# Attention scores of two heads' groups in one pair of PSUM banks: clips, exponentials and additions of 896 elements instead of 448

## The chip, the core and the metric

The kernel runs on one core of one Trainium2 chip. The metric is device time in microseconds (us), the median of several runs. Five engines work side by side, each through its own queue in order: TensorE (PE in the profile, with its weight loads as PEld), VectorE (DVE), ScalarE (ACT), GpSimd (POOL) and SyncE (SP), which here only starts transfers. Matmul results land in PSUM, in eight banks of 512 fp32 elements per partition; DVE and ACT read them from there.

## The reference

Two transformer layers over 8 sequences of 112 tokens, 512 wide, with a context of 375 positions for each sequence:

```python
x = x + _L0_xattn_ref(_layernorm(x), ctx_2048, ctx_2048, mask_bool)
x = x + _L0_ffn_ref(_layernorm(x), w1, w2, w3)
x = x + _L1_xattn_ref(_layernorm(x), ctx_2048, mask_int, Wq, bq, Wk, ...)
x = x + _L1_ffn_ref(_layernorm(x), wq_gate, s_gate, wq_up, s_up, ...)
```

The change is in the third line, the second layer's attention with 16 heads of 32:

```python
q, k, v = proj(hs, Wq, bq), proj(at, Wk, bk), proj(at, Wv, bv)
scores = jnp.clip(jnp.einsum('bhsd,bhtd->bhst', q, k) / sqrt(32), -50, 50)
scores = jnp.clip(jnp.where(attend, scores, -10000.0), -50, 50)
probs = softmax(scores)
delta = rs * (einsum('bhst,bhtd->bhsd', probs, v) @ Wo.T + bo)
```

followed by a layer norm of delta with gamma and beta. The mask is applied by the upper bound of the clip: 50 where a position counts, -50 where it doesn't.

## The kernel before

The kernel goes through four parts: the first attention and first feed-forward (up to about 212 us of the profiled span), the queries of the second attention (to 236), the second attention (236 to 396), and the second feed-forward (to the end). TensorE and SP run in the order in which the program is written throughout; in the attention stage all five engines do.

**Keys and values** of a sequence come in seven steps, each one fill of a bank by TensorE (L194 for keys, L203 for values) and a copy out of it (L197, L205 on ACT in this stage). The generator `key_value_steps` hands them out one at a time, and `fill` puts one behind each step of the attention as other work for TensorE. They use `ps_mm`, a pool of two banks, which the projection (L800) and the turning of its result (L841) use too.

**One step of the attention** is a batch `b` (8 of them) and a third `c` of the 375 positions, 125 each. `scores` takes four banks, one for each of four 32-row groups of the array, `r`; each holds four heads' groups (`dc`) of 112 columns, 448 elements. The matmuls (L902) go `dc` outside, `r` inside. For each bank, DVE clips it into a tile in SBUF (L907) and ACT takes the exponential in place (L908). The four banks are the whole of the pool `ps_s`, so the next step's matmuls need the banks that this step's clips free.

**Sums.** One step later `sums` multiplies the exponentials with the values (L928, into the one bank `num`). The softmax's denominators need the exponentials summed over all 375 positions: POOL adds the second third's to the first's in place (L894, in `add`; on DVE for the last batch), at the start of step `c == 2`, and matmuls with ones take the sum of that and of the last third (L923, into `den`). Then ACT copies both out (L934, L935), and in the next batch's step `c == 1` `divide` takes the reciprocal (L939) and multiplies (L941) on DVE, behind that step's clips.

**Projection and normalisation** of token block `b - 2` follow at `c == 2`: L800 on TensorE, then on DVE and POOL a chain (L806, L143 and on, `rsqrt_pool` at L102 to L109, L812, L813, L819, L821 to L824) whose last part runs before the clips of the next batch's steps. L834 and L841 turn the normalised block for the second feed-forward. Beside this, integer weights arrive by DMA in pieces of 640 columns in two buffers (`load_integers`) and are converted by ACT (L877) and POOL (L879) in `convert_integers`, at set steps, ahead of the exponentials in ACT's queue; a buffer is free for the next DMA when POOL is done.

**Other users of `ps_s`.** In the queries, `less` (L741, read by DVE at L745) and the turning of normalised blocks (L227, `transpose2`); in the second feed-forward, `gate` and `up` (L1031), a bank each for 128 of 1408 hidden rows: ACT reads `gate` (L1036), DVE multiplies with `up` (L1037), and TensorE is two such blocks of rows ahead at most, since there are four banks. In that part the order on DVE, ACT and POOL is the scheduler's.

Of the kernel before, what the change touches and what calls it, by code (L numbers as in the profile page):

```python
# [23 lines left out]
F32 = mybir.dt.float32  # L24
# [6 lines left out]
ALU = mybir.AluOpType  # L31
AX = mybir.AxisListType
PSUM = bass.MemoryType.PSUM
ENGINES = mybir.EngineType

P = 128
B, T, D = 8, 112, 512
KC = D // P
S2, CK = 375, 125
NCK = S2 // CK  # L40
# [3 lines left out]
GROUPS = [(0, 4), (4, 7)]  # L44
HD = 32
NR = P // HD
# [10 lines left out]
CLIP = 50.0 / SC1  # L57
# [7 lines left out]

SPLIT = 2.0 ** -12
LESS = 1.0 - 2.0 ** -13


@with_exitstack  # L70
def two_layers(ctx: ExitStack, tc: tile.TileContext, x, ctxT, ctxN, mask0, mask1, w1, w2, w3,
               wq, wk, wv, wo, bq, bk, bv, bo, gamma, beta, rscale,
               wg, sg, wu, su, wd, sd, out):
    nc = tc.nc
# [72 lines left out]
    def normaliser(srcs, name):  # L147

        mv = moments(srcs, name)
        r = srcs[0].shape[0]  # L150
        ve = small[-1].tile([P, len(srcs)], F32, name=f"{name}_ve", bufs=1)[:r]
        nc.vector.tensor_scalar_add(ve, mv[:, :, 1], LN_EPS)
        rstd = rsqrt(ve, name)

        def write(h, j):
            nc.vector.tensor_scalar(h, srcs[j], mv[:, j, 0:1], rstd[:, j:j + 1],
                                    ALU.subtract, ALU.mult)
        return write
# [59 lines left out]
    def write2(i, write, j, pool):  # L218
        h2[i] = pool.tile([P, D], F32, name="d", bufs=2)
        write(h2[i], j)  # L220

    def transpose2(i, psum):

        g = 0 if i < GROUPS[0][1] else 1
        pt = psum.tile([P, KC, P], F32, name="s")
        for kc in range(KC):
            nc.tensor.transpose(pt[:, kc, :], h2[i][:, kc * P:(kc + 1) * P], ident)  # L227
        j = i - GROUPS[g][0]
        high, low, diff = (t[:, :, j * P:(j + 1) * P] for t in h2T[g])
        nc.scalar.activation(high, pt, AF.Identity, scale=LESS)  # L230

        def end():
            nc.vector.tensor_sub(low, pt, high.bitcast(F32))
            nc.vector.scalar_tensor_tensor(diff, high.bitcast(F32), SPLIT, low.bitcast(F32),
                                           ALU.mult, ALU.subtract)
        return end


    with tc.tile_pool(name="w0", bufs=1, side="right") as w0p, \
# [290 lines left out]
        with tc.tile_pool(name="work1", bufs=2, side="right") as work1:  # L530
# [90 lines left out]
            for i in range(2, NT):  # L621
# [51 lines left out]
                elif i == 4:  # L673
# [3 lines left out]
                                                 for name in ("wq_high", "wq_low", "h2T_high"))  # L677
                    nc.scalar.activation(wq_high, wq_s, AF.Identity, scale=LESS)
                    nc.gpsimd.tensor_sub(wq_low, wq_s, wq_high.bitcast(F32))
# [22 lines left out]

    tailp = ctx.enter_context(tc.tile_pool(name="tailp", bufs=1, side="right"))

    ps_s = ctx.enter_context(tc.tile_pool(name="ps_s1", bufs=4, space=PSUM))
    ps_mm = ctx.enter_context(tc.tile_pool(name="ps_mm1", bufs=2, space=PSUM))
    kv_psum[0] = ps_mm

# [11 lines left out]
    upper = tailp.tile([CK, NCK, B], F32, name="upper")  # L720
# [44 lines left out]
    with tc.tile_pool(name="g1p", bufs=1, side="right") as g1p:  # L765
        h2T[1] = [g1p.tile([P, KC, 384], F32R, name=f"h2T1_{k}") for k in range(3)]
        write = normaliser(xs[4:6], "ln2b")
        for i in range(4, 6):
            write2(i, write, i - 4, tailp)
            transpose2(i, ps_s)()  # L770
        next(asking)
        write2(6, normaliser(xs[6:], "ln2c"), 0, tailp)
        transpose2(6, ps_s)()
        for g in range(2):
            for _ in asking:
                pass
            asking = queries(1)
# [59 lines left out]
    def transpose4(i, pool, name):  # L837

        pt = pool.tile([P, KC, P], F32, name=name)
        for kc in range(KC):  # L840
            nc.tensor.transpose(pt[:, kc, :], h4[i][:, kc * P:(kc + 1) * P], ident)  # L841
        j = i - GROUPS[0 if i < GROUPS[0][1] else 1][0]
        hi, lo = (h4T[k][:, :, j * P:(j + 1) * P] for k in range(2))
        nc.scalar.copy(hi, pt)
        return lambda: nc.vector.tensor_sub(lo, pt, hi.bitcast(F32))


    with tc.tile_pool(name="work2", bufs=1, side="right") as work2, \
# [21 lines left out]
        def convert_integers():  # L870
            for raw, which, half, c, n in loaded:
# [12 lines left out]

        sets = [[work2.tile([P, KC, T], F32, name=f"e{i}{r}") for r in range(NR)]
                for i in range(NCK)]

        def add(b):  # L890
            add = (nc.gpsimd if b in ADD_POOL else nc.vector).tensor_add
            for r in range(NR):
                e, e1 = (sets[(b + c) % NCK][r][:CK] for c in range(2))
                add(e, e, e1)  # L894

        def scores(b, c):
            kT = kvs_of[b][0]
            ss = [ps_s.tile([CK, KC, T], F32, name="s") for r in range(NR)]
            for dc in range(KC):
                for r in range(NR):  # L900
                    rows = slice(r * HD, (r + 1) * HD)
                    nc.tensor.matmul(ss[r][:, dc, :], lhsT=kT[rows, dc, c * CK:(c + 1) * CK],  # L902
                                     rhs=qT[rows, dc, b * T:(b + 1) * T], start=True, stop=True)
            es = sets[(b + c) % NCK]
            for r in range(NR):
                e = es[r][:CK]
                nc.vector.tensor_scalar(e, ss[r], upper[:, c, b:b + 1], -CLIP, ALU.min, ALU.max)  # L907
                nc.scalar.activation(e, e, AF.Exp, scale=SC1)  # L908
            return es

# [37 lines left out]
        for b in range(B):  # L950
            for c in range(NCK):
                if c == 2 and b in ADD_POOL:
                    add(b)
                if (b, c) in due:
                    convert_integers()
                    if counts:
                        load_integers(counts.pop(0))
                es = scores(b, c)
                if c == 2 and b not in ADD_POOL:
                    add(b)  # L960
                if c < STEPS[b]:
                    fill(1)
                if c == NCK - 1:
                    sums(*last)
                if (b, c) == (B - 1, NCK - 1):
                    over = tailp.tile([P, 29], F32, name="over")
                    nc.gpsimd.tensor_scalar(over, squares, WIDE, 1.0, ALU.is_gt, ALU.mult)
                if b == 0 and c > 0:
                    next(folding)
                if c == 0:  # L970
                    while later:
                        later.pop()()
                    if b >= 3:
                        project_end(b - 3)
                elif c == 1 and b >= 1:
                    divide(b - 1)
                elif c == 2:
                    turned = 3 <= b < 3 + GROUPS[0][1]
                    if turned:
                        write4(b - 3)  # L980
                    if b >= 2:
                        project_product(b - 2)
                    if b == B - 1:

                        hits = ps_s.tile([1, 29], F32, name="s")
                        nc.tensor.matmul(hits, lhsT=ones[:, :1], rhs=over, start=True, stop=True)
                        wide = tailp.tile([1, 1], I32, name="wide")
                        nc.vector.tensor_reduce(wide, hits, AX.X, ALU.max)
                    if b >= 2:
                        project_begin(b - 2)  # L990
                    if turned:
                        later.append(transpose4(b - 3, ps_mm, "mm"))
                if last and c < NCK - 1:
                    sums(*last)
                last = b, c, es
# [8 lines left out]
    with tc.tile_pool(name="work3", bufs=2, side="right") as work3, \  # L1004
# [49 lines left out]
        def feed_forward1():  # L1054
            gus = [work3.tile([P, HC, 512], F32R, name=f"gu_{k}", bufs=1) for k in range(2)]
            gate_up1(0, 0, 2, gus)
            project(NT - 1)
            gate_up1(0, 2, HC, gus)
            for i in range(*GROUPS[0]):
                if GROUPS[1][0] + i < NT:  # L1060
                    write4(GROUPS[1][0] + i)
                down1(0, i, gus)
                if GROUPS[1][0] + i < NT:
                    transpose4(GROUPS[1][0] + i, ps_s, "s")()
            gus = [work3.tile([P, HC, 512], F32R, name=f"gu_{k}", bufs=1) for k in range(2)]
            gate_up1(1, 0, HC, gus)
            for i in range(*GROUPS[1]):
                down1(1, i, gus)

        def feed_forward1_wide(g):  # L1070
# [27 lines left out]
            for i in range(i0, i1):  # L1098
# [5 lines left out]
                                     start=(hc == 0), stop=(hc == HC - 1))  # L1104
                finish(i, ps)

        is_wide = nc.values_load(wide[0:1, 0:1], min_val=0, max_val=P)
        with tc.If(is_wide == 0) as fits:
            feed_forward1()
        with fits.Else():  # L1110
            project(NT - 1)
            feed_forward1_wide(0)
            for i in range(*GROUPS[1]):
                write4(i)
                transpose4(i, ps_s, "s")()
            feed_forward1_wide(1)


def _laid_out(inputs):
# [63 lines left out]
```

## Time and profile before

| what | us |
|---|---|
| median of 3 runs (517.44 to 518.0) | 517.8 |
| the profiled execution, its own time | 517.36 |
| its span in the profile | 515.6 |

Busy time of the engines by stretch, from the windows of the trace (us):

| stretch | length | PE | DVE | ACT | POOL |
|---|---|---|---|---|---|
| 200 to 236, queries | 36 | 35.18 | 25.53 | 14.11 | 6.06 |
| 236 to 260 | 24 | 23.69 | 13.65 | 17.17 | 8.06 |
| 260 to 280 | 20 | 19.87 | 13.88 | 14.13 | 8.04 |
| 280 to 300 | 20 | 20.00 | 13.04 | 8.82 | 8.82 |
| 320 to 340 | 20 | 19.02 | 17.80 | 11.80 | 11.69 |
| 340 to 360 | 20 | 20.00 | 16.15 | 11.74 | 12.89 |
| 360 to 380 | 20 | 19.46 | 17.40 | 12.74 | 14.08 |
| 380 to 400 | 20 | 19.78 | 16.43 | 10.62 | 8.17 |

A busy TensorE in such a row is not TensorE at its peak: a matmul's record lasts until its modelled end, so a wait in the middle of a group shows as a group that lasts longer than its like, not as idle time. A line of the profile names the line of the program, the engine, the operation, the tiles written and read with their shapes, and the number of instructions; what follows depends on the view and is said there. The granted TensorE clock is 1.00 in all of these stretches.

### The profile page before, as it was taken

Reading aid. Unit: us, or ns where it says so; the run is one execution under the profiler, and the core shown is the slowest. Engines: PE = TensorE matmul, PEld = TensorE weight load, DVE = VectorE, ACT = ScalarE, POOL = GpSimd, SP = SyncE. Lnnn points to the kernel's source line nnn. Section 1 sums busy time; section 2 is a strip of 40 time slices with the busy share of each in tenths; the row PEclk is TensorE's granted clock in tenths of the full one; section 3 lists DMA queues with packets and bytes.
Section 4 is the critical chain, followed back from the end, with each engine's and each line's share of the span. In section 5 each row is a group of like instructions: output and inputs, shape, how many; then the busy total and the mean of one; then the engine's idle time right before and its main releaser. Section 6 shows DMA issues by size and latency. Waiting matters only on the chain.

```text
span 515.6 us, 8804 instructions
## 1 busy us (share of the span) xinstructions
PE 502.3 (97%) x3380; PEld 315.0 (61%) x3380; DVE 334.3 (65%) x801; ACT 252.4 (49%) x438; POOL 133.9 (26%) x221
## 2 busy tenths in 40 slices
PE   9999999999999999999999999999999999999995
PEld 6445554455545455686565465555555788889983
DVE  3642548767798986964676588997897753334432
ACT  0326656857565665336675375465665233103310
POOL 0000121110011164211551475574753430000000
PEclk9999999999999999999999999999999999999998
DMA  8997795200120100122421112012320000010001
GB/s 242 363 407 298 274 326 201 79 18 0 61 82 1 60 2 0 37 109 58 162 70 53 61 52 62 3 53 62 98 76 5 21 1 1 20 42 20 1 20 46
DMA packets 13343, 45.75 MB, mean 89 GB/s; under 512 B 2081, under 2 KB 3120, under 8 KB 12144
## 3 DMA queue, kind: packets, MB, share of 16 engines
q1 hardware_dynamic: 11744, 41.43, 23.4%
q0 software_dynamic: 1248, 3.70, 2.2%
q8 instruction: 28, 0.46, 0.4%
q14 instruction: 19, 0.16, 0.1%
q10 hardware_dynamic: 304, 0.01, 0.0%
HBM read 41.46 MB, written 1.84 MB: 84 GB/s over the span
## 4 chain that ended last, share of the span: by engine, by line
PE 47%; DVE 6%; POOL 2%; DMA 1%; ACT 1%; issue 1%; DVEq 0%; POOLq 0%
PE s L1031 14%; PE mm L203 8%; PE down L1049 7%; PE mm L800 4%; PE s L902 3%; PE num L928 2%; PE mm L194 2%; DVE e L907 2%; PE den L923 2%; DMA raw<-in_wd_dram 1%; PE mm L737 1%; PE mm L735 1%; PE s L741 1%; DVE e L939 1%; POOL ln_t L108 1%
## 5 line engine op out<-in xcount | busy, mean ns | idle before, releaser
L194 PE MATMUL mm<-cT,wk 128*128 128x375 f32 x256 | 87.6, 487 | 0.0
L203 PE MATMUL mm<-wv,cT 128*125 128x512 f32 x192 | 87.6, 599 | 0.0
L1031 PE MATMUL s<-h4T,w 128*128 128x512 f32 (+1 forms) x352 | 72.6, 367 | 0.2 <-PE num L928 0.2
L1031 PEld LDWEIGHTS s<-h4T,w 128*128 128x128 f32 x352 | 63.5, 188 | 8.8 <-PE num L928 0.5
L907 DVE TENSOR_SCALAR e<-s,upper 125x448 f32<-125x448 f32 x96 | 59.0, 676 | 14.7 <-PE s L902 13.9
L908 ACT ACTIVATE e<-e 125x448 f32<-125x448 f32 x96 | 51.7, 570 | 27.6 <-DVE e L907 27.0
L194 PEld LDWEIGHTS mm<-cT,wk 128*128 128x128 f32 x256 | 47.0, 191 | 27.6 <-issue 0.8
L203 PEld LDWEIGHTS mm<-wv,cT 128*125 128x125 f32 x192 | 34.5, 187 | 38.0 <-issue 36.4
L894 POOL TENSOR_TENSOR e<-e,e 125x448 f32<-125x448 f32 x28 | 33.7, 1233 | 14.9 <-PE num L928 14.9
L1049 PE MATMUL down<-w,gu 128*128 128x512 f32 x154 | 37.0, 396 | 0.0
L541 PE MATMUL mm<-w_q,q_qT 128*128 128x512 fp8e4 (+1 forms) x168 | 34.6, 361 | 1.5 <-ACT q_qT L352 1.1
L439 POOL DMA_DIRECT2D tokens<-x x14 | 10.7, 768 | 90.6 <-DVE x L433 64.0
L1049 PEld LDWEIGHTS down<-w,gu 128*128 128x128 f32 x154 | 28.6, 188 | 6.7
L1039 ACT CAST gu<-gu 128x512 fp32r<-128x512 f32 (+1 forms) x22 | 12.5, 567 | 39.6 <-DVE gu L1037 39.6
L877 ACT ACTIVATE w<-raw,zero_point 128x640 fp32r<-128x640 int32 (+2 forms) x29 | 22.6, 781 | 18.9 <-DMA raw<-in_wd_dram 7.6
L570 POOL TENSOR_SCALAR q<-gu 128x704 bf16<-128x704 f32 x14 | 10.8, 787 | 80.0 <-ACT gu L567 80.0
L902 PE MATMUL s<-qT,kv 32*125 32x112 f32 x768 | 29.3, 280 | 0.6 <-DVE qT L745 0.3
L1037 DVE SCALAR_TENSOR_TENSOR gu<-s,su,gu 128x512 f32<-128x512 f32 (+1 forms) x22 | 15.0, 684 | 21.9 <-PE s L1031 20.6
L902 PEld LDWEIGHTS s<-qT,kv 32*125 32x125 f32 x768 | 24.5, 183 | 7.1 <-issue 5.6
L541 PEld LDWEIGHTS <-q_qT 128*128 128x128 bf16 x168 | 16.4, 98 | 20.3 <-issue 1.8
L879 POOL TENSOR_SCALAR w<-raw 128x640 fp32r<-128x640 int32 (+2 forms) x29 | 19.8, 693 | 34.2 <-ACT w L877 33.9
L800 PE MATMUL mm<-wo,qT 128*128 128x512 f32 x56 | 25.8, 603 | 1.0 <-DVE qT L941 1.0
(236 smaller groups left out, 787.5 us busy)
## 6 DMA issues: line engine op xcount, KB each, us to landing
cT<-in_ctxT_dram SPq DMA_DIRECT2D x13, 750.0 KB, 6.1
raw<-in_w_dram SPq DMA_DIRECT2D x6, 1408.0 KB, 19.2
cN<-in_ctxN_dram SPq DMA_DIRECT2D x8, 768.0 KB, 4.4
raw<-in_wg_dram SPq DMA_DIRECT2D x8, 320.0 KB, 3.1
raw<-in_wu_dram SPq DMA_DIRECT2D x8, 320.0 KB, 3.0
raw<-in_wd_dram SPq DMA_DIRECT2D x8, 320.0 KB, 3.1
out_dram<-d SPq DMA_DIRECT2D x7, 256.0 KB, 2.0
wk<-in_wk_dram SPq DMA_DIRECT2D x4, 256.0 KB, 4.8
```

What stands on the lines that cost most here:

```text
L194: nc.tensor.matmul(ps[dc], lhsT=wk_s[:, kc, dc * P:(dc + 1) * P], rhs=cT[:, kc, :], start=(kc == 0), stop=(kc == KC - 1))
L203: nc.tensor.matmul(ps, lhsT=cT[:, kc, c * CK:(c + 1) * CK], rhs=wv_s[:, kc, :], start=(kc == 0), stop=(kc == KC - 1))
L541: nc.tensor.matmul(ps[:, :n], lhsT=qT[:, kc, :], rhs=w[:, kc * H + n0:kc * H + n0 + n], start=(kc == 0), stop=(kc == KC - 1))
L800: nc.tensor.matmul(ps, lhsT=qT[:, kc, i * P:(i + 1) * P], rhs=wo_s[:, kc, :], start=(kc == 0), stop=(kc == KC - 1))
L877: nc.scalar.activation(t, raw, AF.Square, bias=zero_point, accum_out=squares[:, k:k + 1])
L879: nc.gpsimd.tensor_scalar(t, raw, -128.0, 1.0, ALU.add, ALU.mult)
L894: add(e, e, e1)
L902: nc.tensor.matmul(ss[r][:, dc, :], lhsT=kT[rows, dc, c * CK:(c + 1) * CK], rhs=qT[rows, dc, b * T:(b + 1) * T], start=True, stop=True)
L907: nc.vector.tensor_scalar(e, ss[r], upper[:, c, b:b + 1], -CLIP, ALU.min, ALU.max)
L908: nc.scalar.activation(e, e, AF.Exp, scale=SC1)
L1031: nc.tensor.matmul(ps[:, :n], lhsT=w[:, c:c + P], rhs=h4T[k][:, kc, :n], start=(kc == 0 and k == 0), stop=(kc == KC - 1 and k == 1))
L1049: nc.tensor.matmul(ps, lhsT=gus[k][:, hc, j * P:(j + 1) * P], rhs=w[:, c:c + D], start=(hc == 0 and k == 0), stop=(hc == HC - 1 and k == 1))
```

## The change

Two PSUM banks become one tile, a pair, and `ps_s` becomes a pool of two pairs in place of four banks. In `scores`, rows groups 0 and 1 go into one pair, 2 and 3 into the other; the matmuls and their order stay. One clip, one exponential and one addition take a pair, 896 elements. The exponentials' tiles are laid out in twos to match, and single heads' parts of them are views. Counts fall from 96 to 48 clips and exponentials, from 28 to 14 additions on POOL and from 4 to 2 on DVE.

Everything else that used `ps_s` asks a small class `Halves`, which takes a pair from the pool and hands out its two banks one after the other. There are two of them, one for `less`, `gate` and `up`, one for turned blocks; a half that is left over is dropped at the border of a stage. A pair is free for its next user when all that read either half are done.

```diff
+class Halves:
+    def __init__(self, pool):
+        self.pool, self.left = pool, []
+
+    def tile(self, shape, dtype, name):
+        if not self.left:
+            pair = self.pool.tile([P, 2, 512], F32, name="s")
+            self.left = [pair[:, 0, :], pair[:, 1, :]]
+        n = 1
+        for d in shape[1:]:
+            n *= d
+        t = self.left.pop(0)[:shape[0], :n]
+        return t if len(shape) == 2 else t.rearrange("p (a b) -> p a b", a=shape[1])
...
-    ps_s = ctx.enter_context(tc.tile_pool(name="ps_s1", bufs=4, space=PSUM))
+    ps_pair = ctx.enter_context(tc.tile_pool(name="ps_s1", bufs=2, space=PSUM))
+    ps_s, ps_turned = Halves(ps_pair), Halves(ps_pair)
...
-            transpose2(i, ps_s)()
+            transpose2(i, ps_turned)()
...
-        sets = [[work2.tile([P, KC, T], F32, name=f"e{i}{r}") for r in range(NR)]
+        twos = [[work2.tile([P, 2, KC, T], F32, name=f"e{i}{h}") for h in range(NR // 2)]
                 for i in range(NCK)]
+        sets = [[two[r // 2][:, r % 2] for r in range(NR)] for two in twos]
+        ps_turned.left.clear()
 
         def add(b):
             add = (nc.gpsimd if b in ADD_POOL else nc.vector).tensor_add
-            for r in range(NR):
-                e, e1 = (sets[(b + c) % NCK][r][:CK] for c in range(2))
+            for h in range(NR // 2):
+                e, e1 = (twos[(b + c) % NCK][h][:CK] for c in range(2))
                 add(e, e, e1)
 
         def scores(b, c):
             kT = kvs_of[b][0]
-            ss = [ps_s.tile([CK, KC, T], F32, name="s") for r in range(NR)]
+            ss = [ps_pair.tile([P, 2, 512], F32, name="s") for h in range(NR // 2)]
             for dc in range(KC):
                 for r in range(NR):
                     rows = slice(r * HD, (r + 1) * HD)
-                    nc.tensor.matmul(ss[r][:, dc, :], lhsT=kT[rows, dc, c * CK:(c + 1) * CK],
+                    nc.tensor.matmul(ss[r // 2][:CK, r % 2, dc * T:(dc + 1) * T], lhsT=kT[rows, dc, c * CK:(c + 1) * CK],
                                      rhs=qT[rows, dc, b * T:(b + 1) * T], start=True, stop=True)
-            es = sets[(b + c) % NCK]
-            for r in range(NR):
-                e = es[r][:CK]
-                nc.vector.tensor_scalar(e, ss[r], upper[:, c, b:b + 1], -CLIP, ALU.min, ALU.max)
+            for h in range(NR // 2):
+                e = twos[(b + c) % NCK][h][:CK].rearrange("p a k t -> p a (k t)")
+                nc.vector.tensor_scalar(e, ss[h][:CK, :, :KC * T], upper[:, c, b:b + 1], -CLIP,
+                                        ALU.min, ALU.max)
                 nc.scalar.activation(e, e, AF.Exp, scale=SC1)
-            return es
+            return sets[(b + c) % NCK]
...
-                        hits = ps_s.tile([1, 29], F32, name="s")
+                        hits = Halves(ps_pair).tile([1, 29], F32, name="s")
...
-                    transpose4(GROUPS[1][0] + i, ps_s, "s")()
+                    transpose4(GROUPS[1][0] + i, ps_turned, "s")()
...
+        for halved in ps_s, ps_turned:
+            halved.left.clear()
```

More of the change, by code (lines that the diff above doesn't have):

```diff
@@ L769, in two_layers @@
             write2(i, write, i - 4, tailp)
-            transpose2(i, ps_s)()
+            transpose2(i, ps_turned)()
         next(asking)
         write2(6, normaliser(xs[6:], "ln2c"), 0, tailp)
-        transpose2(6, ps_s)()
+        transpose2(6, ps_turned)()
         for g in range(2):
@@ L1109, in two_layers @@
             feed_forward1()
+            for halved in ps_s, ps_turned:
+                halved.left.clear()
         with fits.Else():
@@ L1114, in two_layers @@
                 write4(i)
-                transpose4(i, ps_s, "s")()
+                transpose4(i, ps_turned, "s")()
             feed_forward1_wide(1)
+            for halved in ps_s, ps_turned:
+                halved.left.clear()
 def _laid_out(inputs):
```

## The prediction

> **What bounds the kernel now.** I read the page's busy shares first, then the windows by stage, then TensorE's own timeline through the attention stage, and last the timelines of the engines it waits for. The page:
>
> ```profile
> PE 502.3 (97%) x3380; PEld 315.0 (61%) x3380; DVE 334.3 (65%) x801; ACT 252.4 (49%) x438; POOL 133.9 (26%) x221
> L907 DVE TENSOR_SCALAR e<-s,upper 125x448 f32<-125x448 f32 x96 | 59.0, 676 | 14.7 <-PE s L902 13.9
> L908 ACT ACTIVATE e<-e 125x448 f32<-125x448 f32 x96 | 51.7, 570 | 27.6 <-DVE e L907 27.0
> L894 POOL TENSOR_TENSOR e<-e,e 125x448 f32<-125x448 f32 x28 | 33.7, 1233 | 14.9 <-PE num L928 14.9
> ```
>
> TensorE is busy nearly all the time, and its work does not change: no matmul is added or dropped. So the change can pay only where TensorE stands still for one of these three groups. They lie at 236 to 396 us. TensorE's timeline there (start, length, engine, line) has one step as it normally runs and the steps that run long or start late:
>
> ```profile
> 263.28 1.14 PE L902 MATMUL s<-qT,kv 32*125 32x112 f32 x32
> 267.98 1.96 PE L902 MATMUL s<-qT,kv 32*125 32x112 f32 x32
> 301.64 1.77 PE L902 MATMUL s<-qT,kv 32*125 32x112 f32 x32
> 325.87 3.70 PE L800 MATMUL mm<-wo,qT 128*128 128x512 f32 x8 [0.98 <-DVE qT L941]
> 362.31 1.46 PE L902 MATMUL s<-qT,kv 32*125 32x112 f32 x32
> 371.56 0.65 PE L841 MATMUL mm<-ident,d 128*128 128x128 f32 x4 [0.54 <-ACT kv L197]
> ```
>
> Against 1.14 us the three long score steps lose 0.82, 0.63 and 0.32 us. With 0.98 and 0.54 that is 3.3 us, and two waits at the stage's ends (0.31 and 0.22) that the change doesn't reach. This is the ceiling. What the long score steps wait for is in the weight loads' timeline:
>
> ```profile
> 268.82 0.94 PEld L902 LDWEIGHTS s<-qT,kv 32*125 32x125 f32 x26 [0.30 <-DVE e L907]
> ```
>
> Six of 32 records (three heads; each fp32 matmul leaves two) go out, and the fourth head's bank waits for the **last** clip of the step before. The three places are those where DVE comes to its clips late, behind the reciprocal (L939, 2.94 us) and the divide (L941), or behind the normalisation's chain.
>
> **Clips (L907).** Four of 448 elements take 2.46 us from first start to last end: 0.676 alone, so a new one starts each (2.46 - 0.676)/3 = 0.595. What more elements cost is in L745's two shapes, 690 ns at 512 and 553 at 384: 1.07 ns each. A clip of 896 starts 0.595 + 0.48 = 1.07 after the one before and lasts 1.15, so two take 2.22 us. Taken: 0.25 us saved per set. Ends: no fixed part saved, 0; or 0.27 if elements cost 1.04 ns.
>
> **Exponentials (L908).** Unpaced by clips, four take 1.96 us: one each 0.463. L877's 640 and 256 element forms (828 and 510 ns) give 0.83 ns an element, so a pair takes 0.463 + 0.37 = 0.83 more and lasts 0.94: 1.77 us. Saved 0.19. Where clips pace them, the first pair starts 0.47 later than the first single did, and the last ends 2.22 + 0.94 = 3.16 after the first clip's start against 2.46 + 0.57 = 3.03: 0.13 later. The products (L928) use them one step later; the tightest is at 323.91, with exponentials ending at 322.83, so 0.13 is covered by 1.08.
>
> A rule of the Trainium skill speaks against this (Perfetto Trace Analysis, Optimizing Scalar/DVE Operations): larger operations help a saturated engine, but where an engine is not saturated and causes bubbles, instructions should be broken up so that some work is done sooner. The windows (us, then TensorE, weight loads, DVE, ACT, POOL) read in most of this stage:
>
> ```profile
> 300.00:320.00 20.00, 19.87 (x243) 11.78 (x242) 17.32 (x30) 11.54 (x24) 13.94 (x25) 1.00 0.23 71
> ```
>
> DVE at 17 of 20 us is not saturated, and it causes the bubbles. By the rule each bubble would grow by the 0.47 us that the first result comes later: 3 x 0.47 = 1.4 us lost. The row of 26 records decides otherwise: TensorE waits for the last bank, and the last clip ends earlier. Only if TensorE had reached the first bank before its clip would the rule hold, and DVE's lateness in these rows is 0.3 to 0.8 us against a set of 2.46.
>
> **Additions (L894) and the divide.** POOL adds twice 896 elements instead of four times 448, on seven batches. One takes 1.13 us, and L813 (512 elements) 1.28: 2.3 ns an element, so 896 cost 2.15, and the next starts 0.04 before the end. Ends: 1.92, if an element costs twice L879's one-input 0.88 ns; 2.26, doubled. POOL itself gains some 0.1 to 0.3 us, and nobody waits for it. But the divide (L941) waits for an addition in progress:
>
> ```profile
> 265.24 0.96 DVE L941 TENSOR_TENSOR qT<-qT,e 128x448 f32<-128x448 f32 x1
> 264.58 1.13 POOL L894 TENSOR_TENSOR e<-e,e 125x448 f32<-125x448 f32 x1
> 265.67 1.51 POOL L894 TENSOR_TENSOR e<-e,e 125x448 f32<-125x448 f32 x1
> 325.18 0.63 DVE L941 TENSOR_TENSOR qT<-qT,e 128x448 f32<-128x448 f32 x1
> ```
>
> Ready at 265.24 it ends at 266.20, 0.53 after POOL's second addition gave way at 265.67; the third then takes 1.51. All six divides beside additions end 0.5 to 0.6 after such a boundary. The Trainium skill has the rule (SBUF — State Buffer, Who interferes with whom): a DVE instruction with two SBUF inputs and a GpSimd one share a port pair, and whoever starts first holds it for the whole instruction. The hold therefore grows from 1.09 to 2.11 us. Counting from POOL's first addition, divides are ready at 1.75, 0.85, 1.52, 2.14, 1.11 and 1.48 us (batches 1 to 6), and 0.25 earlier after the change: 1.50, 0.60, 1.27, 1.89, 0.86, 1.23. All fall into the first double addition and end 2.11 + 0.55 after its start. That is where five of them end already (boundary at 2.18); batch 2 ends 1.0 us later (boundary 1.09 now), hidden because its projection starts only at 287.11, three us later. So the lock swallows most of the gain that the clips make ahead of a divide. Without the lock the divide at 265.24 would end 0.6 earlier.
>
> **The sum.**
> - 267.98: divide 0.07 earlier, then the clips behind it 0.25 shorter: 0.32 of 0.82.
> - 301.64: clips start as now (their start hangs on POOL's L813), end 0.25 earlier: 0.25 of 0.63.
> - 325.87: the divide ends at 323.04 + 2.11 + 0.55 = 325.70 against 325.81: 0.11.
> - 362.31 and 371.56 are one item. The second wait hangs on a chain that starts at the projection of 347.34: normalisation, POOL's conversion (L879), a DMA issued at 364.13 that lands 4.1 us later, conversion, exponentials, key copy (L197). What TensorE gains at 362.31 it waits longer at 371.56; only the exponentials' 0.19 shortens the chain.
>
> Together 0.87 us. **Other stages.** Banks are now freed by pairs. In the query stage the tightest pair is freed by DVE's L745 at 228.00, asked for at 228.61. In the last feed-forward a gate product now waits for L1037 of two blocks back instead of L1036: mostly 2.4 us free, at the tightest 0.57 (L1037 at 417.81 ends 418.56, the gate starts 419.13). If that cover goes, the excess is paid one to one. Their cost is taken as nothing. The profiled execution took 517.36 us, its span 515.6; the median shown is 517.8, 0.4 above it. Taking 0.87 from the median: **516.9 us**.
>
> **Rivals.**
> - *The lock does not matter* (additions shorter or placed differently): the divides keep the clips' gain, and the stall at 267.98 goes wholly. 0.82 + 0.25 + 0.26 + 0.19 = 1.5: 516.3 us. For it: the clips do end earlier. Against: six divides of six show the lock.
> - *The divide misses its window* (slower). In batch 4 it is ready 1.89 after POOL's start, and the first addition gives way at 2.11: 0.22 of room. An addition under 1.93 us, or clips that save less than 0.03, lets POOL's second addition in first. Batch 5 shows such a loss: ready 0.02 after a boundary, it waited a whole addition. It would end at 2 x 2.11 + 0.55 = 4.77 instead of 2.77, and the projection at 325.87 waits 2.0 us more. With the other gains (0.76) that is 1.2 us slower, 519.0; with a short addition (1.9) 518.6, with no clip gain 519.5.
> - *The gate waits*: DVE's order in the last feed-forward is the scheduler's; L1037 of block 2 behind the wait of L819 (until 415.9) would end 1.2 us after its gate at 415.40. 518.1 us.
> - *It doesn't do what it says*: clips over two banks cost their fixed part twice. Then only the 0.19 and 0.1 remain, unless the window is missed: 517.5.
>
> **How the numbers follow.** Forecast 0.55 (own range 516.4 to 517.4), no lock 0.15, missed window 0.17, gate waits 0.05, no saving 0.03, and 0.05 for a slowdown that I haven't seen. A measurement of this kernel tells about 0.2% from no change, 1.04 us: the borders are 516.76 and 518.84. Four tenths of the forecast's range lie below the first, and the second case does: faster 0.37. The rest of the forecast (0.33), the gate, no saving and the mildest of the missed windows (0.02) are within: 0.43. Slower: 0.15 and 0.05. The range 516.1 to 518.6 takes in all but the missed window's worse part and the unseen.
>
> **What will show it.** 48 clips near 1.15 us, 48 exponentials near 0.94, POOL additions x14 near 2.15; score steps near 268 and 302 at about 1.64 and 1.52 us; divides of batches 1 to 6 all ending 2.6 to 2.7 after POOL's first addition; batch 2's divide near 1.9 us long. A projection wait near 326 of over 2 us, or a wait of a gate product for L1037, makes the prediction wrong.

## The result, and the profile after

The changed kernel takes 519.6 us (median of 6 runs, 519.17 to 520.18), the kernel before 517.84 beside it (6 runs): a ratio of 1.0036, with a 95% interval of 1.0023 to 1.0049. It is 1.8 us slower where 0.9 us faster was forecast, and lies above the range (516.1 to 518.6). The span of the profiled execution went from 515.6 to 517.5 us.

The lines below are shifted: clips are L927, exponentials L929, POOL's additions L915, the divide L962, score matmuls L923, the gate and up matmuls L1052, SiLU L1057, the gate product L1058. The page of the changed kernel, first its busy shares, then three groups (busy us and mean ns of one, then the engine's idle time ahead of them):

```profile
PE 501.9 (97%) x3380; PEld 314.0 (61%) x3380; DVE 330.8 (64%) x751; ACT 245.8 (47%) x390; POOL 132.8 (26%) x207
L927 DVE TENSOR_SCALAR e<-s,upper 125x896 f32<-125x896 f32 x48 | 52.9, 1144 | 15.7 <-PE s L923 13.8
L929 ACT ACTIVATE e<-e 125x896 f32<-125x896 f32 x48 | 44.6, 945 | 34.8 <-DVE e L927 33.0
L915 POOL TENSOR_TENSOR e<-e,e 125x896 f32<-125x896 f32 x14 | 31.4, 2265 | 14.6 <-PE num L949 12.7
```

Half as many instructions. Clips and exponentials have the length that was forecast (1.15 and 0.94 us). An addition that nothing holds up takes 2.08 us, forecast 2.15; the mean in the row is longer, because a second one takes longer where a divide gets in ahead of it (2.46 in batch 4). Each of the three engines is less busy than before. So the wide instructions themselves do what they were meant to do. TensorE's timeline of the attention stage agrees:

```profile
269.71 1.62 PE L923 MATMUL s<-qT,kv 32*125 32x112 f32 x32
303.03 1.53 PE L923 MATMUL s<-qT,kv 32*125 32x112 f32 x32
326.84 3.70 PE L818 MATMUL mm<-wo,qT 128*128 128x512 f32 x8 [0.80 <-DVE qT L962]
363.27 1.23 PE L923 MATMUL s<-qT,kv 32*125 32x112 f32 x32
372.06 0.66 PE L859 MATMUL mm<-ident,d 128*128 128x128 f32 x4 [0.30 <-ACT kv L214]
```

Against before the five places are shorter by 0.34, 0.24, 0.18, 0.23 and 0.24 us, 1.23 in all. (Two of the experiments below, `whole_pair` and `dve_order`, run the same attention code. Their profiles repeat the first four to 0.03 us, but have 0.58 and 0.38 us for the fifth, the wait at 372. So its 0.24 is not shown to be the change's.) The time is lost elsewhere. I cut the span at three starts on TensorE: the first query matmul (L753), the first score row that follows a wait, and the first gate matmul:

| stage (us) | before | after | difference |
|---|---|---|---|
| up to the queries | 214.43 | 214.45 | +0.02 |
| queries | 21.92 | 23.62 | +1.70 |
| attention | 160.44 | 159.14 | -1.30 |
| second feed-forward | 118.81 | 120.29 | +1.48 |

In the profiles of `whole_pair` and `dve_order` the attention takes 159.42 and 159.25 us, so its gain is 1.0 to 1.3 us.

**The queries' loss** is one place in TensorE's timeline. Before, two blocks were turned in one go:

```profile
220.18 1.03 PE L227 MATMUL s<-ident,d 128*128 128x128 f32 x8
```

After:

```profile
220.20 0.60 PE L244 MATMUL s<-ident,d 128*128 128x128 f32 x4
222.27 0.65 PE L244 MATMUL s<-ident,d 128*128 128x128 f32 x4 [1.47 <-DVE h2T L250]
```

Blocks 4 and 5 now have the two halves of one pair, and block 5's transposes wait for L250, DVE's reading of block 4's half, which ends at 222.21. DVE's timeline after:

```profile
221.53 0.68 DVE L250 TENSOR_TENSOR h2T<-s,h2T 128x512 fp32r<-128x512 f32 x1
```

The two blocks go to different banks; what joins them is the tile. The wait is 1.47 us, and the two rows last 1.25 us against 1.03 in one, which together is the 1.70.

**The feed-forward's loss** is one wait too. TensorE's timeline before, then after:

```profile
407.38 34.16 PE L1031 MATMUL s<-h4T,w 128*128 128x512 f32 x144
```

```profile
407.80 8.03 PE L1052 MATMUL s<-h4T,w 128*128 128x512 f32 x32
417.04 26.40 PE L1052 MATMUL s<-h4T,w 128*128 128x512 f32 x112 [1.22 <-DVE gu L1058]
```

From the first start to the last end the 144 matmuls now take 35.64 us, 1.48 more than before: the stage's whole loss. They wait for the gate product of two blocks of rows earlier. ScalarE's and then DVE's timeline after show why that is late:

```profile
412.18 0.69 ACT L1057 ACTIVATE gu<-s,sg 128x512 f32<-128x512 f32 x1 [3.25 <-PE s L1052]
```

```profile
415.57 0.75 DVE L837 SCALAR_TENSOR_TENSOR tokens<-d,ln_f,tokens 128x512 f32<-128x512 f32 x1 [2.88 <-POOL ln_f L830]
416.24 0.75 DVE L1058 SCALAR_TENSOR_TENSOR gu<-s,su,gu 128x512 f32<-128x512 f32 x1
```

And ScalarE's and DVE's timelines before:

```profile
409.90 0.69 ACT L1036 ACTIVATE gu<-s,sg 128x512 f32<-128x512 f32 x1 [1.40 <-PE s L1031]
```

```profile
412.19 0.75 DVE L1037 SCALAR_TENSOR_TENSOR gu<-s,su,gu 128x512 f32<-128x512 f32 x1
415.15 0.75 DVE L819 SCALAR_TENSOR_TENSOR tokens<-d,ln_f,tokens 128x512 f32<-128x512 f32 x1 [2.21 <-POOL ln_f L812]
```

The same two instructions of DVE stand in the opposite order. The product could have begun when the SiLU ended, at 412.87; instead it stands behind an addition that waits 2.88 us for a factor from POOL. The SiLU itself begins at 412.18 where it began at 409.90 before (the stage starts 0.42 us later): it reads `gate`, and now waits until the matmuls of `up` are done, in the other half.

### The profile page after: what moved, and what is told of

The parts are those of the page before. It is cut to its first block, busy times and chain, and to the rows that moved or that the text cites. A ratio compares the mean times of both kernels' runs of the same rounds, so it can differ in the third digit from the quotient of the medians.

```text
span 517.5 us, 8635 instructions
## 1 busy us (share of the span) xinstructions
PE 501.9 (97%) x3380; PEld 314.0 (61%) x3380; DVE 330.8 (64%) x751; ACT 245.8 (47%) x390; POOL 132.8 (26%) x207
## 4 chain that ended last, share of the span: by engine, by line
PE 49%; DVE 5%; DMA 1%; POOL 1%; ACT 1%; issue 1%; DVEq 0%; POOLq 0%; SPq 0%
PE s L1052 11%; PE mm L220 8%; PE down L1070 7%; PE mm L211 5%; PE s L923 4%; PE mm L818 4%; PE num L949 3%; PE den L944 2%; PE mm L755 1%; PE mm L753 1%; PE s L759 1%; DVE e L960 1%; DMA raw<-in_wd_dram 1%; DMA sd<-in_sd_dram 1%; POOL ln_t L125 0%
## 5 line engine op out<-in xcount | busy, mean ns | idle before, releaser
L1052 PE MATMUL s<-h4T,w 128*128 128x512 f32 (+1 forms) x352 | 72.8, 367 | 1.4 <-DVE gu L1058 1.2
L1052 PEld LDWEIGHTS s<-h4T,w 128*128 128x128 f32 x352 | 63.5, 188 | 10.3 <-DVE gu L1058 1.7
L927 DVE TENSOR_SCALAR e<-s,upper 125x896 f32<-125x896 f32 x48 | 52.9, 1144 | 15.7 <-PE s L923 13.8
L929 ACT ACTIVATE e<-e 125x896 f32<-125x896 f32 x48 | 44.6, 945 | 34.8 <-DVE e L927 33.0
L915 POOL TENSOR_TENSOR e<-e,e 125x896 f32<-125x896 f32 x14 | 31.4, 2265 | 14.6 <-PE num L949 12.7
L1057 ACT ACTIVATE gu<-s,sg 128x512 f32<-128x512 f32 (+1 forms) x22 | 13.9, 634 | 35.9 <-PE s L1052 31.2
L1058 DVE SCALAR_TENSOR_TENSOR gu<-s,su,gu 128x512 f32<-128x512 f32 (+1 forms) x22 | 15.0, 683 | 24.0 <-ACT gu L1057 22.8
L923 PE MATMUL s<-qT,kv 32*125 32x112 f32 x768 | 28.8, 279 | 0.3 <-DVE qT L763 0.3
L923 PEld LDWEIGHTS s<-qT,kv 32*125 32x125 f32 x768 | 24.0, 183 | 6.7 <-issue 5.6
L949 PEld LDWEIGHTS num<-e,kv 125*32 125x32 f32 x768 | 18.4, 110 | 13.6 <-issue 7.9
```

What stands on the lines that cost most here:

```text
L923: nc.tensor.matmul(ss[r // 2][:CK, r % 2, dc * T:(dc + 1) * T], lhsT=kT[rows, dc, c * CK:(c + 1) * CK], rhs=qT[rows, dc, b * T:(b + 1) * T ...
L927: nc.vector.tensor_scalar(e, ss[h][:CK, :, :KC * T], upper[:, c, b:b + 1], -CLIP, ALU.min, ALU.max)
L949: nc.tensor.matmul(num[r * HD:(r + 1) * HD, dc, :], lhsT=v[:, c, head], rhs=es[r][:CK, dc, :], start=(c == 0 and dc == 0), stop=(c == NCK ...
L1052: nc.tensor.matmul(ps[:, :n], lhsT=w[:, c:c + P], rhs=h4T[k][:, kc, :n], start=(kc == 0 and k == 0), stop=(kc == KC - 1 and k == 1))
```

## The experiments

My theory: the attention gains 1.3 us, and the halves of the two other stages lose 3.2, in the queries because two turned blocks share a tile, in the feed-forward through DVE's order. Rivals: the wide instructions hand time on to later stages; the loss is the pairs' release and not the sharing or the order; the pools' new places or chance in the schedule. Ratios are against runs of the kernel before, on the same chip (median 517.3 to 517.5). By its ratio the changed kernel would stand at 519.3 there.

### Pairs in one stage at a time

Four kernels give one stage or more a pool of its own. In `att_only`:

```diff
-    ps_pair = ctx.enter_context(tc.tile_pool(name="ps_s1", bufs=2, space=PSUM))
-    ps_s, ps_turned = Halves(ps_pair), Halves(ps_pair)
     ps_mm = ctx.enter_context(tc.tile_pool(name="ps_mm1", bufs=2, space=PSUM))
+    ps_q = ExitStack()
+    ps_s = ps_turned = ps_q.enter_context(tc.tile_pool(name="ps_s1", bufs=4, space=PSUM))
...
     queried.close()
+    ps_q.close()
...
     with tc.tile_pool(name="work2", bufs=1, side="right") as work2, \
+            tc.tile_pool(name="ps_s2", bufs=2, space=PSUM) as ps_pair, \
...
     with tc.tile_pool(name="work3", bufs=2, side="right") as work3, \
+            tc.tile_pool(name="ps_s3", bufs=4, space=PSUM) as ps_s, \
```

`q_single` has the first of these pools and pairs from the attention on, `ff_single` the last and pairs up to there, `not_att` pairs in the outer stages and the attention's code of before.

> The pairs are used in the attention alone; queries and last feed-forward take single banks as before the change. If the attention's part gains what its stage shows (1.3 us) and the two other stages lose 1.7 and 1.5 us through the halves: 516.5 us, with no wait of TensorE for L250's subtraction at 222 us and none of 1.2 us for a gate product at 417 us. If instead the attention's wider instructions lose time that only shows up later: 518 us or more, since the rest is as before.

> As changed, but the queries take single banks again. If the turned blocks 4 and 5 hold each other up as halves of one tile, and this costs 1.7 us: 517.9 us, the turning of block 5 follows that of block 4 without a wait, and the wait of 1.2 us at 417 us stays. If the queries' loss is from the order of the pools or from chance in the schedule: 519.6 us.

> As changed, but the last feed-forward takes single banks again. If the pairs cost the feed-forward 1.5 us: 518.1 us, the SiLU again begins under the second product, the wait of 1.2 us at 417 us is gone and the wait of about 1.5 us at 222 us stays. If the feed-forward's loss was handed on by the attention (a late last block): 519.6 us.

> The other way round: queries and last feed-forward take halves of pairs, the attention's scores and additions are as before the change. If the losses are these two stages' own: 517.8 + 1.7 + 1.5 = 521.0 us, with both waits (222 and 417 us). If they come of the attention's wider instructions: 517.8 us.

| kernel | median us | ratio, 95% interval |
|---|---|---|
| att_only | 517.57 | 1.0004 (0.9994 to 1.0014) |
| q_single | 519.75 | 1.0042 (1.0026 to 1.0059) |
| ff_single | 519.22 | 1.0034 (1.0025 to 1.0043) |
| not_att | 521.75 | 1.0079 (1.0063 to 1.0096) |

Three of the four are 0.8 to 1.1 us above what my theory says, q_single 1.9. Every one has a wait that neither kernel has. TensorE's timeline of `att_only`:

```profile
216.07 0.47 PE L753 MATMUL mm<-h2T_high,wq_high 128*128 128x512 f32 x1 [0.89 <-issue]
```

I had opened `ps_mm` first. My reading was that it so got the banks which the stage before had used for its own `mm` until just then. The next three kernels move it. (In q_single a further 0.9 us over the theory shows in the timed runs and not in the profile; where it lay stays open.)

### The same, with `ps_mm` at the other end of PSUM

```diff
-    ps_mm = ctx.enter_context(tc.tile_pool(name="ps_mm1", bufs=2, space=PSUM))
+    ps_mm = ctx.enter_context(tc.tile_pool(name="ps_mm1", bufs=2, space=PSUM, side="right"))
```

> As att_only, with the projections' two banks at the other end of PSUM, so that the queries' first products don't get banks in use until just before (att_only's new wait of 0.89 us at 216.07). If that wait and the longer one at the attention's start (0.72 for 0.31 us) are the price of where the banks lie: 517.57 - 0.9 - 0.4 = 516.3 us, faster than before by about 1.2 us. If the pairs in the attention bring nothing: 517.5 us.

> As q_single, with the projections' banks at the other end. If the halves of the queries cost 1.7 us and nothing else differs from the changed kernel: 519.6 - 1.7 = 517.9 us, with the wait of 1.2 us at 417 us. If single banks in the queries bring nothing: 519.6 us.

> As ff_single, with the projections' banks at the other end. If the halves of the last feed-forward cost 1.5 us: 519.6 - 1.5 = 518.1 us, with the waits of 0.8 and 1.5 us for L250 kept. If they cost nothing: 519.6 us.

| kernel | median us | ratio, 95% interval | queries | attention | feed-forward |
|---|---|---|---|---|---|
| att_only_r | 516.6 | 0.9985 (0.9978 to 0.9991) | 21.92 | 159.45 | 118.93 |
| q_single_r | 518.04 | 1.0014 (1.0006 to 1.0023) | 21.92 | 159.35 | 120.35 |
| ff_single_r | 518.31 | 1.0023 (1.0014 to 1.0032) | 23.62 | 159.56 | 118.85 |

The wait of 0.89 us is gone, and all three lie within 0.3 us of the theory's numbers. So the place of the pool made it; that it was the earlier use of these banks is likely and not shown, since the row ("issue") names no releaser. The wait at the attention's start, which I had put down to the same cause, stays at 0.72 us in `att_only_r`: that part was wrong. In these three profiles a stage's length follows that stage's own banks: queries with single banks take 21.92 us, with halves 23.62, whatever follows, and the feed-forward with single banks 118.93 and 118.85 behind a paired attention. So the wide instructions hand nothing on. In `att_only_r` both waits are gone from TensorE's timeline:

```profile
219.85 1.03 PE L244 MATMUL s<-ident,d 128*128 128x128 f32 x8
...
406.04 34.15 PE L1054 MATMUL s<-h4T,w 128*128 128x512 f32 x144
```

It is faster than both kernels: 0.8 us below the one before, and about 2.7 below the changed one by the latter's ratio.

### What in the queries: the shared tile

`whole_pair` leaves the changed kernel as it is, but drops the left half ahead of each turned block, so that no two share a pair:

```diff
+            ps_turned.left.clear()
             transpose2(i, ps_turned)()
```

> As changed, but each of the turned blocks 4, 5 and 6 of the queries takes a pair of its own, with the other half left empty. If the wait of 1.47 us is from two blocks sharing a tile: it goes, and the time is 519.6 - 1.5 = 518.1 us, unless the pairs, now asked for more often, are not yet free, for which a new wait would stand at 220 to 229 us. If the wait is from the pair's release by an earlier user: it stays, 519.6 us.

518.3 us, ratio 1.0020 (1.0009 to 1.0031). TensorE's timeline:

```profile
220.77 0.60 PE L244 MATMUL s<-ident,d 128*128 128x128 f32 x4
221.78 0.66 PE L244 MATMUL s<-ident,d 128*128 128x128 f32 x4 [0.41 <-DVE qT L763]
```

The wait for block 4's reader is gone. A shorter one takes its place, for L763, which frees the second pair of another user. The queries take 22.56 us: of the 1.70 lost, 1.06 goes with the sharing. Of the 0.64 left, 0.41 is this wait for a pair that is asked for before it is free, and the rest is that two rows last 1.26 us where one lasts 1.03. The two intervals overlap a little; it is the stage's length that separates the kernels.

### What in the feed-forward: the order on DVE

`dve_order` keeps the halves, the SiLU's wait and the place of every matmul, and writes DVE's order out by hand:

```diff
-            project(NT - 1)
-            gate_up1(0, 2, HC, gus)
+            with tc.manual_schedule(engines={ENGINES.PE, ENGINES.SP, ENGINES.DVE}):
+                project_product(NT - 1)
+                project_begin(NT - 1)
+                gate_up1(0, 2, 3, gus)
+                project_end(NT - 1)
+                gate_up1(0, 3, HC, gus)
```

> As changed, with the halves everywhere, but VectorE's order in the last feed-forward's first group is the written one: the product of block 2 (L1058) stands ahead of the addition L837 that waits for GpSimd's factor, as it did before the change. If the wait of 1.22 us at 417 us comes from that order: it goes, the attention's gain and the queries' loss stay, 519.3 - 1.2 = 518.1 us. If the pair's release or the SiLU's wait for the second product makes it by itself: it stays, 519.3 us.

518.26 us, ratio 1.0013 (1.0004 to 1.0022). DVE's timeline, and then TensorE's:

```profile
413.19 0.75 DVE L1058 SCALAR_TENSOR_TENSOR gu<-s,su,gu 128x512 f32<-128x512 f32 x1
...
416.22 0.75 DVE L837 SCALAR_TENSOR_TENSOR tokens<-d,ln_f,tokens 128x512 f32<-128x512 f32 x1 [0.90 <-POOL ln_f L830]
```

```profile
408.08 34.16 PE L1052 MATMUL s<-h4T,w 128*128 128x512 f32 x144
```

The product ends at 413.94 instead of 416.99 and TensorE no longer waits. The feed-forward takes 118.81 us, to the hundredth that of before. So the whole 1.48 is the order; the coarser release and the late SiLU alone cost nothing here. (The edit fixes DVE's order in the whole of this group of rows, not of the two instructions alone.) That the scheduler changed the order because the SiLU became later is the likely reason; no run shows it.

### Which of the three wide instructions pays

Three kernels start from `att_only_r` and put back one of them. `clip_single` (`exp_single` does the same with the exponential, `add_single` loops over the four row groups in `add`):

```diff
-                nc.vector.tensor_scalar(e, ss[h][:CK, :, :KC * T], upper[:, c, b:b + 1], -CLIP,
-                                        ALU.min, ALU.max)
+                for k in range(2):
+                    nc.vector.tensor_scalar(e[:, k], ss[h][:CK, k, :KC * T], upper[:, c, b:b + 1], -CLIP,
+                                            ALU.min, ALU.max)
```

> As att_only_r (516.6), but each clip covers one head's group again, exponentials and additions stay paired. If the clips' widening gives 0.25 us at each score step that TensorE waits for: the steps near 268, 302, 325, 362 and 371 us are 0.25 us longer and the time is 517.4 to 517.8. If the clips give nothing and the gain is from elsewhere: 516.6 us.

> As att_only_r (516.6), but each exponential covers one head's group again; clips and additions stay paired. Two singles take 0.98 us where the pair takes 0.94, and both begin after the same clip: 0.04 us at each of five steps, 516.6 to 516.8 us by the theory that the clips pace the set. If ScalarE paces it (0.19 us a set): 517.0 to 517.6 us.

> As att_only_r (516.6), but GpSimd's additions take one head's group each again (four a batch). If the boundary between two long additions costs or saves VectorE's divide as the prediction has it: the waits behind the divide (L819 at 326 us) become 0.1 to 0.2 us longer, 516.7 to 516.8 us. If the paired additions delay the divide for nothing: about 0.5 us faster, 516.1 us.

| kernel | median us | ratio, 95% interval | attention |
|---|---|---|---|
| clip_single | 520.79 | 1.0056 (1.0037 to 1.0074) | 163.97 |
| exp_single | 517.38 | 0.9996 (0.9983 to 1.0010) | 159.44 |
| add_single | 516.61 | 0.9982 (0.9974 to 0.9990) | 159.88 |

**The clips** are worth more than expected: with single ones the median is 4.2 us above that of `att_only_r`, and the attention of the profile 4.5 us longer. The three score steps account for 1.0 (0.33, 0.36, 0.35). The rest is at the projection, in TensorE's timeline of `clip_single`:

```profile
327.65 5.40 PE L819 MATMUL mm<-wo,qT 128*128 128x512 f32 x8 [2.83 <-DVE qT L963]
```

Two things are in this row. The wait is 2.83 us against 0.80, because the divide missed the gap between POOL's two additions. POOL's and DVE's timelines of `clip_single`, a fence each:

```profile
323.00 4.12 POOL L915 TENSOR_TENSOR e<-e,e 125x896 f32<-125x896 f32 x2 [0.70 <-PE num L950]
```

```profile
325.12 2.48 DVE L963 TENSOR_TENSOR qT<-qT,e 128x448 f32<-128x448 f32 x1
```

Ready 2.12 us after POOL's start, just behind the middle of the two additions (2.06), it ended with the second, at 4.60. With wide clips, in the changed kernel, it is ready 1.86 us after POOL's start and gets through. Then the eight matmuls take 5.40 us instead of 3.70. The windows of `clip_single` (us, then TensorE, weight loads, DVE, ACT, POOL, and the granted TensorE clock) show why:

```profile
324.00:327.60 3.60, 0.82 (x32) 0.58 (x25) 3.49 (x2) 0.00 (x0) 3.12 (x2) 1.00 0.00 0
327.60:330.00 2.40, 2.35 (x5) 1.12 (x6) 2.30 (x4) 0.95 (x1) 0.00 (x0) 0.80 0.00 0
330.00:333.00 3.00, 3.00 (x7) 1.16 (x6) 0.62 (x2) 0.95 (x1) 0.00 (x0) 0.59 0.00 0
```

After the long wait the clock is no longer whole. Its mean over the last two rows is 0.68, and 0.68 of 5.40 us is 3.69, the length of these matmuls at the full clock. 2.03 of waiting and 1.70 of slower clock, with the 1.0 above, make 4.7 us; 0.2 comes back at the next wait (0.27 for 0.49), which leaves the 4.5.

Two things limit this reading. Of the 13 timed executions six took 518.87 to 519.32 us, at a mean clock of 0.996 or 0.997; seven took 520.79 to 522.64, at 0.991 to 0.995. The profile is of one of the seven. The six have no profile; by their mean clock they lose none, and they lie about 1.7 us below the profiled one, which is what the clock cost there. So single clips cost about 2.5 us where the clock stays whole. And this is the price of single clips together with long additions. The kernel before has single clips too, and its attention is only about 1.0 us longer than that of `att_only_r`: there the divide is ready 2.14 us after POOL's start, 0.04 ahead of a boundary between two short additions, and gets through.

**The exponentials** bring almost nothing in the attention stage. TensorE's timeline of `exp_single`, whose three long steps are 1.62, 1.53 and 1.21 us in `att_only_r`:

```profile
269.00 1.67 PE L923 MATMUL s<-qT,kv 32*125 32x112 f32 x32
302.37 1.54 PE L923 MATMUL s<-qT,kv 32*125 32x112 f32 x32
362.61 1.22 PE L923 MATMUL s<-qT,kv 32*125 32x112 f32 x32
```

They lose 0.05, 0.01 and 0.01 us. The kernel's median is 0.8 us above that of `att_only_r`, in the range that I had given to the rival that ScalarE sets the pace. But the stage has the same length (159.44 and 159.45), the two intervals overlap, and the profile loses 1.3 us ahead of the queries (they start at 215.43 instead of 214.10), at loads of the first stage that this edit doesn't touch:

```profile
5.63 10.33 PE L211 MATMUL mm<-cT,wk 128*128 128x375 f32 x32 [0.81 <-DMA wk<-in_wk_dram]
...
20.83 3.70 PE L220 MATMUL mm<-wv,cT 128*125 128x512 f32 x8 [0.71 <-DMA wv<-in_wv_dram]
```

**The additions** decide no measurable time (516.61 against 516.6), though the stage of the profile is 0.4 us longer. The small effect expected at the projection is there: it waits 0.92 us for 0.80. POOL's timeline of `add_single`, then DVE's:

```profile
322.57 4.80 POOL L915 TENSOR_TENSOR e<-e,e 125x448 f32<-125x448 f32 x4 [0.68 <-PE num L949]
```

```profile
324.45 0.83 DVE L962 TENSOR_TENSOR qT<-qT,e 128x448 f32<-128x448 f32 x1
```

The divide ends 2.71 us after POOL's start, behind the second of four short additions, where it ends 2.57 after the start behind one long one.

## Why the prediction was wrong

- **TensorE is the bound, the ceiling is its five waits: right.** 1.23 of the attention's 1.30 us came from exactly those five. The forecast 0.87 was 0.2 to 0.4 too low: the same attention gained 1.02 and 1.19 in `whole_pair` and `dve_order`.
- **Clips: right.** 1144 ns against 1.15, a set in 2.21 us (2.20 to 2.21 in `att_only_r`) against 2.22. The rule to break instructions up, which names a possibility and no must, would by the prediction's sum have had the wide ones lose 1.4 us; the long score steps became shorter, and with single clips put back they are 0.33 to 0.36 us longer.
- **Exponentials: length right (945 ns), worth wrong.** The 0.19 us at 362 and 371 was put down to them; `exp_single` keeps the gain at 362 (1.22 us), and `clip_single` loses it (1.56), so there it is the clips'. Whether the two places are one item, as the prediction had it, stays open. In the changed kernel both waits shrank (0.23 and 0.24 us). But the second is anything from 0.30 to 0.58 us in the kernels with the same attention where it shows, and in `clip_single` it gave back 0.22 of the 0.35 lost at the first, as the prediction said.
- **Additions and the lock: right.** All six divides end 2.56 or 2.57 us after POOL's first addition, forecast 2.66: the boundary comes at 2.05 and not 2.11. Two of them, in POOL's and in DVE's timeline after:

```profile
283.14 4.50 POOL L915 TENSOR_TENSOR e<-e,e 125x896 f32<-125x896 f32 x2 [9.36 <-PE num L949]
...
324.21 4.51 POOL L915 TENSOR_TENSOR e<-e,e 125x896 f32<-125x896 f32 x2 [0.72 <-PE num L949]
```

```profile
283.71 1.99 DVE L962 TENSOR_TENSOR qT<-qT,e 128x448 f32<-128x448 f32 x1
...
326.07 0.71 DVE L962 TENSOR_TENSOR qT<-qT,e 128x448 f32<-128x448 f32 x1
```

  Batch 2's divide lasts 1.99 us (forecast 1.9) and nobody waits for it; batch 4's keeps 0.2 us of room (ready at 1.86). The prediction's "0.6 earlier" without the lock has the clips' 0.25 in it: a divide beside no addition takes 0.62 us (before, at 385.83), so from 265.24 alone it is 0.34.
- **Rival "the divide misses its window": not here**, but `clip_single` is it, with the forecast price (2.0 us; measured 2.03) and one that no row of before showed, the clock (1.70).
- **"Other stages. ... Their cost is taken as nothing": this step failed.** The queries lost 1.70 us and the feed-forward 1.48. The step asked only when a whole pair comes free, on the timeline of before.
  - For the queries it compared L745's 228.00 with 228.61, and did not ask what the two owners of one pair's halves do to each other: a wait of 1.47 us. Undoing the sharing wins back 1.06; then a pair's release does cost 0.41. No rival had this loss.
  - For the feed-forward it kept DVE's order of before. In that order the product that failed has room: it ended at 412.94 and its gate began at 415.40, and in `dve_order`, with halves, it still ends in time (413.94). The halves cost nothing there; the new order put the product behind an addition that waits for POOL. The rival "the gate waits" had the mechanism, the instruction, the addition ahead of it and the price (1.2 us; 1.22 measured as idle time, 1.48 with the rows' restart), and its wait was named among the signs of being wrong. Its chance of 0.05 was too low for an order that a scheduler decides anew.

## What to carry to other kernels

When two buffers become one tile, ask in every stage that uses them which readers and writers of the one half now order those of the other, not only when the whole comes free. Where an engine's order is a scheduler's, an order read from the old trace is no cover: put the two candidates in both orders and price the worse. And put the wide tiles only where the wide instructions are: pairs in the attention alone, with `ps_mm` at the other end of PSUM, turn a loss of 0.36% into a gain of 0.15%.

## What the runs showed of the chip that was not expected

In one profile a wait of 2.83 us of TensorE was followed by a granted clock of 0.80 and 0.59 over the next 5.4 us, so that a late divide cost nearly twice its own lateness. Six of that kernel's 13 executions kept a mean clock of 0.996 or 0.997, so the loss does not come every time. The waits of 0.8 to 1.5 us in the kernels before and after left the clock at 1.00 in the windows read. And which banks a pool gets is not free: the same pools at the other end of PSUM saved 0.89 us of wait where a stage begins.
